# Seven block products for the candidate's input, merged gate tiles, norm sums as side outputs, and some sums on GpSimd

## The chip, the core and the metric

The kernel runs on one core of a Trainium2 chip. The metric is the device time of one execution in microseconds (us). Each version is timed several times; the number given is the median. In the profile PE is TensorE (matmuls), PEld its weight loads, DVE is VectorE, ACT is ScalarE, POOL is GpSimd and SP the engine that issues most DMAs.

## The reference, cut to what matters

The input x has 128 graphs of 64 nodes with 256 features, with a 64x64 adjacency matrix per graph. Four layers follow each other, and each ends in `x = layernorm(x + layer(x))`:

- Layer 0 is a gated graph network of five steps. In each step the node states h are multiplied by a message weight and summed over neighbours (agg), and a gated cell updates h:

```
r = sigmoid(i_r + h_r);  z = sigmoid(i_z + h_z)
n = tanh(i_n + r * h_n)
h = (1 - z) * n + z * h
```

  The i parts are products of agg with the input weights, the h parts are products of h with the state weights. n is called the candidate here.
- Layer 1 sums neighbours, multiplies by W1 (256x1024), divides by the root mean square, applies silu, and multiplies by W2 (1024x256).
- Layer 2 maps x to a tangent space (a logarithm of the norm), sums neighbours, and maps back (a tanh of the norm).
- Layer 3 is an attention with exponentials.

Everything is fp32.

## The kernel before, in words

**Tiling.** Two graphs share the 128 partitions (a block); four blocks make a group of 512 rows, and there are 16 groups. Three sets of work buffers exist (NF = 3), so about three groups are in flight. In layer 0 features lie on partitions, and h and agg are tiles of 128 x 2 x 512: two halves k of the features, and two halves n of the rows (256 columns each).

**Layer 0.** The message weight is multiplied into the input weight beforehand, in the setup, so that a step aggregates h itself (`agg_of`: transposes of h into row layout, a copy hr, the product with the adjacency, a copy agg). The gate products (`gate`) and the state part of the candidate (`state_side`) are 2x2 block products, done with seven block multiplications in the place of eight: sums and differences of weight blocks are prepared in the setup (`sums_of`, tiles w_h, w_a, w_hn with seven blocks), differences of input blocks are made in each step (`sums`, tiles tA for h and tB for agg), and partial results are combined while they leave PSUM. The input part of the candidate is a plain product: `product` into the banks p_in (L675), four products per half, eight per step, 80 steps in all. A bank of p_in is added to r * h_n on VectorE (L837), tanh follows on ScalarE (L839), and three VectorE instructions make the new state hT (L841, L845, L847). This is done for row half 0 first, and for row half 1 later. The gate values live in four tiles of 128x2x256 (slots U, Z, V, R).

**Layer 1.** Seven block multiplications again (`by_sums`, L938 and L943), except in the last two groups, which use the plain product (`as_it_is`). `square` squares each 128x512 piece on ScalarE (L924) and adds it to sqs on VectorE (L926). GpSimd adds the output bias to x (L909, the tile xb).

**Norms.** `layer_norm` runs bn_stats and bn_aggr on VectorE (L685, L686), a power of -0.5 on GpSimd (L690), and a scale and shift on ScalarE or VectorE.

**Order.** Every instruction is first recorded as an operation (`Op`) with an assumed duration, what it reads and what it writes. `Flow.issue` then chooses the order for each engine: it advances a simple clock for each engine and picks the operation that can start first, with ties broken by one of several rules (`ranks`). The kernel before tries all rules in stretches of 37.5 us (10 us near the end) and keeps the 8 (32) best partial plans. Operations with two `ways` may go to ScalarE or VectorE. The orders found are fixed on each engine's queue; at run time the engines only wait on semaphores. Eight PSUM banks are handed out in that order.

Of the kernel before, what the change touches and what calls it, by code (L numbers as in the profile page):

```python
# [42 lines left out]
class Op:  # L43
    __slots__ = ("eng", "us", "run", "ways", "stream", "n", "kb", "sets", "need", "then", "bufs", "opens", "id", "way")

    def __init__(self, ways, stream, n, kb, sets):
        self.ways = {eng: (us, run) for eng, us, run in ways}
        self.eng, self.us, self.run = ways[0]
        self.stream, self.n, self.kb, self.sets = stream, n, kb, sets
        self.need, self.then, self.bufs, self.opens, self.id, self.way = 0, [], (), None, 0, 0.0  # L50


class Plan:


    def __init__(self, flow):
# [8 lines left out]
        self.left, self.first, self.bus, self.done = len(ops), 0, 0.0, 0.0  # L65
        self.lands = [0.0] * flow.TRANSFERS
        self.past, self.order, self.table = None, [], None

    def copy(self):
        c = Plan.__new__(Plan)  # L70
        c.flow, c.need, c.at, c.uses = self.flow, self.need.copy(), self.at.copy(), self.uses.copy()
        c.clock, c.banks, c.lands = self.clock.copy(), self.banks.copy(), self.lands.copy()
        c.queues = [{e: d.copy() for e, d in q.items()} if self.first <= s < self.first + 2 * self.flow.WINDOW else q
                    for s, q in enumerate(self.queues)]
        c.left, c.first, c.bus, c.done = self.left, self.first, self.bus, self.done
        c.past, c.order, c.table = (self.past, self.order), [], self.table
        return c

    def advance(self, until, rank):
# [3 lines left out]
        while self.left and clock["PE"] < until:  # L83
            best = None
            for s in range(self.first, min(self.first + flow.WINDOW, len(self.queues))):
                for e, q in self.queues[s].items():
                    opened = False
                    for _, o in zip(range(flow.AHEAD[e]), q):
                        t = max(clock[e], at[o.id])
# [24 lines left out]
            if eng == "PE":  # L114
                self.done += o.us
# [20 lines left out]

    def bound(self):

        now = self.clock["PE"]
        end = max(now - self.done + self.flow.work, *self.clock.values())  # L140
        for q in self.queues[self.first:]:
            for d in q.values():
                if d:
                    end = max(end, max(self.at[d[0].id], now) + d[0].way)
        return end


class Flow:
# [23 lines left out]
    WINDOW, STRETCH, WIDTH, LAGS = 4, 37.5, 8, (60.0, 150.0,)  # L172


    ENDGAME, LAST_STRETCH, LAST_WIDTH = 400.0, 10.0, 32
# [10 lines left out]
    def op(self, eng, us, run, w=(), r=(), kb=0, sets=None):  # L186
        self.either([(eng, us, run)], w, r, kb, sets)

    def either(self, ways, w, r, kb=0, sets=None):

        o = Op(ways, len(self.streams) - 1, len(self.ops), kb, sets)
# [36 lines left out]
    def ways(self):  # L228
# [9 lines left out]
        self.work = sum(o.us for ops in self.streams for o in ops if o.eng == "PE")  # L238

    def issue(self):  # L240
        self.ways()
        ranks = (lambda s, o: (s, o.n), lambda s, o: (s if o.kb else -s, o.n), *(lambda s, o, lag=lag: (lag * s - o.way, s, o.n) for lag in self.LAGS))
        plans, until = [Plan(self)], 0.0
        while any(p.left for p in plans):
            late = until > self.work - self.ENDGAME
            until += self.LAST_STRETCH if late else self.STRETCH
            found = {}
            for p in plans:
                for rank in ranks:
                    c = p.copy()  # L250
                    if c.advance(until, rank):
                        found.setdefault((round(c.bound(), 3), c.left), c)
            plans = [found[k] for k in sorted(found)[:self.LAST_WIDTH if late else self.WIDTH]]
        p, parts = plans[0], []
        past = (p.past, p.order)
        while past is not None:
            parts.append(past[1])
            past = past[0]
        last = {}
        for part in reversed(parts):  # L260
            for eng, o in part:
                made = o.ways[eng][1]()
                for i in made if isinstance(made, list) else [made]:
                    if eng in last:
                        self.tc.add_manual_dep(i.ins, last[eng].ins.name, self.BEHIND, reason="the plan's order")
                    last[eng] = i
# [3 lines left out]
def kernel(  # L270
# [79 lines left out]
    def dve(n, run, w, r):  # L350
        flow.op("DVE", 0.145 + 0.00105 * n, run, w, r)
# [11 lines left out]
    def scaled(n, o, i, scale, bias, w, r):  # L363

        flow.either([("ACT", 0.22 + 0.00077 * n, lambda: nc.scalar.activation(o(), i(), AF.Identity, bias=bias(), scale=scale())),
                     ("DVE", 0.145 + 0.00105 * n, lambda: nc.vector.tensor_scalar(o(), i(), scale(), bias(), OP.mult, OP.add))], w, r)

    def pool(us, run, w, r=()):
        flow.op("POOL", us, run, w, r)
# [62 lines left out]
    w_a, w_in = [fixed([P, 7, D], f"w_a_{l}") for l in range(L)], [fixed([P, KD, D], f"w_in_{l}") for l in range(L)]  # L432
# [3 lines left out]
    def sums_of(w, eng, us):  # L436

        v = nc.vector if eng == "DVE" else nc.gpsimd
        for o, x0, x1 in ((ms1, ms4, mn22), (ms3, m11, ms4), (ms2, ms1, m11), (ms4, m12, ms2)):
            flow.op(eng, us, lambda o=o, x0=x0, x1=x1: v.tensor_sub(w[:, o, :], w[:, x0, :], w[:, x1, :]),  # L440
                    [(w, o)], [(w, x0), (w, x1)])
# [9 lines left out]
    vecs = fixed([NC, P], "vecs")  # L451
    nmr = fixed([NBLK, P], "nmr")
    at = 0
    for v, n in ((b_ih, NV), (b_hh, NV), (b1, KH), (rms_w, KH)):
        flow.op("POOL", 0.55, lambda v=v, n=n, at=at: nc.gpsimd.dma_start(
            vecs[at:at + n, :], v.rearrange("(c p) -> c p", p=P)), [(vecs, at)], kb=3)
        at += n
    flow.op("POOL", 0.55, lambda: nc.gpsimd.dma_start(nmr.tile(), nodemask.rearrange("(k t) n -> k (t n)", t=2)),
            [nmr], kb=32)
# [694 lines left out]
```

## Time and profile before

| | |
|---|---|
| time, median of 3 | 2415.85 us (2415.77 to 2416.1) |
| span of the profiled execution | 2413.2 us |
| TensorE busy | 2364.1 us, 12098 instructions |
| weight loads busy | 2071.5 us |
| VectorE busy | 1894.3 us, 4404 instructions |
| ScalarE busy | 1211.1 us, 2549 instructions |
| GpSimd busy | 175.1 us, 144 instructions |
| p_in products (L675) | 1280 instructions of 128x256, 321.3 us busy |

How to read it: an fp32 product of the program appears as two matmul instructions in the profile (the 640 products of p_in give 1280). Matmuls overlap in the pipeline, so the mean duration of one (379 ns) is longer than the distance from one to the next. In lists of groups, `out<-in` names the tiles, then come partitions x elements, the count, the busy time, the mean in ns, and the idle time of the engine just before these instructions with the instruction that ended it. In the timeline the first two columns are start and length in us, and a bracket gives idle time and its releaser.

### The profile page before, as it was taken

What the parts mean: (1) busy time and instruction counts of PE and PEld (TensorE: products, weight loads), DVE (VectorE), ACT (ScalarE), POOL (GpSimd) and SP (SyncE); (2) the same over time, 40 slices, a digit from 0 to 9 for tenths busy, and PEclk for the clock granted to TensorE, in tenths of its full rate; (3) what the DMA queues carried; (4) which work ended last, traced back from release to release, by engine and by line L of the source; (5) the groups of instructions that cost most, each with busy time, mean ns of one, the idle gap of its engine ahead of it and who ended that gap; (6) DMA issues with size and microseconds to landing.
All of it is one profiled execution on the core that took longest, in us unless ns stands there. A gap on an engine that the chain in (4) does not pass through costs nothing.

```text
span 2413.2 us, 32774 instructions
## 1 busy us (share of the span) xinstructions
PE 2364.1 (98%) x12098; PEld 2071.5 (86%) x12098; DVE 1894.3 (78%) x4404; ACT 1211.1 (50%) x2549; POOL 175.1 (7%) x144
## 2 busy tenths in 40 slices
PE   9999999999999999999999999999999999999995
PEld 7888888888888888888888888888888888888764
DVE  5677887878869787887977877878697987888766
ACT  3344554545544555555454455455454544555454
POOL 2000000000000000000000000000010000100001
PEclk9999999999999999999999999999999999999997
DMA  3000000000000000000000000000000000000000
GB/s 121 10 9 3 1 29 1 27 3 1 29 1 29 1 18 12 1 29 1 27 3 1 27 3 4 26 1 29 1 18 12 27 3 1 27 10 18 10 9 18
DMA packets 39727, 36.22 MB, mean 15 GB/s; under 512 B 9956, under 2 KB 38656, under 8 KB 39568
## 3 DMA queue, kind: packets, MB, share of 16 engines
q1 hardware_dynamic: 37840, 32.25, 4.2%
q8 instruction: 96, 1.57, 0.3%
q10 hardware_dynamic: 1328, 1.31, 0.2%
q0 software_dynamic: 400, 0.57, 0.1%
q14 instruction: 63, 0.52, 0.1%
HBM read 25.74 MB, written 8.39 MB: 14 GB/s over the span
## 4 chain that ended last, share of the span: by engine, by line
PE 91%; DVE 6%; ACT 1%; issue 1%; POOL 0%; POOLq 0%; ACTq 0%; DVEq 0%
PE p_v L772 11%; PE p_r L772 11%; PE p_w L772 11%; PE p_in L675 11%; PE ps_o L342 9%; PE ps_agg L342 6%; PE p_hy L783 6%; PE p_u L772 6%; PE p_hx L783 4%; PE ps_hr L655 3%; PE ps_a L342 2%; PE p_wh L938 2%; PE p_vh L938 2%; PE p_1h L938 2%; PE ps_sup L342 1%; PE ps_hid L342 1%
## 5 line engine op out<-in xcount | busy, mean ns | idle before, releaser
L675 PE MATMUL p_in<-agg,w_in 128*128 128x256 f32 x1280 | 321.3, 379 | 0.0
L675 PEld LDWEIGHTS p_in<-agg,w_in 128*128 128x128 f32 x1280 | 242.2, 190 | 33.9 <-issue 1.0
L342 PE MATMUL ps_o<-w2s,hid 128*128 128x256 f32 x1024 | 234.0, 381 | 4.8 <-ACT hid L998 4.8
L342 PEld LDWEIGHTS ps_o<-w2s,hid 128*128 128x128 f32 x1024 | 193.8, 191 | 32.4 <-ACT hid L998 5.9
L690 POOL TENSOR_TENSOR rstd<-ve,pow 128x4 f32<-128x4 f32 (+1 forms) x64 | 83.6, 1306 | 1407.3 <-DVE ve L688 1401.3
L826 ACT ACTIVATE V<-V,half_b 128x256 f32<-128x256 f32 x160 | 73.3, 500 | 195.4 <-DVE V L822 195.4
L772 PE MATMUL p_v<-tA,w_h 128*128 128x256 f32 x640 | 170.0, 379 | 0.5 <-DVE V L822 0.5
L772 PE MATMUL p_r<-hT,w_h 128*128 128x256 f32 x640 | 168.5, 379 | 0.0
L772 PE MATMUL p_v<-tB,w_a 128*128 128x256 f32 x640 | 167.1, 379 | 0.0
L772 PE MATMUL p_r<-agg,w_a 128*128 128x256 f32 x640 | 167.0, 380 | 0.0
L794 DVE SCALAR_TENSOR_TENSOR hnb<-p_hy,half_b,hs 128x256 f32<-128x256 f32 x240 | 108.6, 478 | 46.1 <-PE p_hy L783 45.2
L342 PEld LDWEIGHTS ps_agg<-edge,hr 128*128 128x128 f32 x1024 | 136.8, 191 | 8.2 <-ACT hr L360 0.5
L342 PE MATMUL ps_agg<-edge,hr 128*128 128x128 f32 x1024 | 138.7, 275 | 0.0
L360 ACT COPY agg<-ps_agg 128x512 f32<-128x512 f32 x154 | 89.1, 579 | 98.7 <-PE ps_agg L342 98.2
L360 ACT COPY hr<-ps_hr 128x512 f32<-128x512 f32 x125 | 72.2, 578 | 128.2 <-PE ps_hr L655 127.7
L772 PEld LDWEIGHTS p_v<-tB,w_a 128*128 128x128 f32 x640 | 120.7, 190 | 16.1 <-DVE tB L759 0.2
L772 PEld LDWEIGHTS p_r<-agg,w_a 128*128 128x128 f32 x640 | 119.1, 190 | 15.9 <-issue 0.5
L772 PEld LDWEIGHTS p_v<-tA,w_h 128*128 128x128 f32 x640 | 118.4, 190 | 15.9 <-DVE V L822 1.4
L783 PE MATMUL p_hy<-tA,w_hn 128*128 128x256 f32 x480 | 131.3, 380 | 0.0
L772 PEld LDWEIGHTS p_r<-hT,w_h 128*128 128x128 f32 x640 | 116.6, 190 | 14.0 <-PE ps_hr L655 0.5
L826 ACT ACTIVATE Z<-Z,half_b 128x256 f32<-128x256 f32 x160 | 73.8, 503 | 93.4 <-DVE Z L822 93.2
L826 ACT ACTIVATE U<-U,half_b 128x256 f32<-128x256 f32 x160 | 73.3, 500 | 88.9 <-DVE U L822 88.4
(242 smaller groups left out, 5346.9 us busy)
## 6 DMA issues: line engine op xcount, KB each, us to landing
x<-in_x_dram SPq DMA_DIRECT2D x16, 512.0 KB, 3.6
xr<-in_x_dram SPq DMA_DIRECT2D x16, 512.0 KB, 3.5
out_dram<-x_n SPq DMA_DIRECT2D x16, 512.0 KB, 2.9
edge<-in_adj_dram SPq DMA_DIRECT2D x32, 64.0 KB, 2.3
wm<-in_L_gnn_weight_dram SPq DMA_DIRECT2D x5, 256.0 KB, 5.3
w2s<-in_L_gnn_W_dram SPq DMA_DIRECT2D x1, 1024.0 KB, 9.1
w<-in_L_gnn_W_dram SPq DMA_DIRECT2D x2, 512.0 KB, 3.4
w_in_L_gnn_w_hh_dram<-in_L_gnn_w_hh_dram ACTq DMA_DIRECT2D x1, 512.0 KB, 5.2
```

The source lines that it names most:

```text
L342: return nc.tensor.matmul(o, lhsT, rhs, start=(k == 0), stop=(k == nk - 1))
L360: flow.either([("ACT", 0.22 + 0.00077 * n, lambda: nc.scalar.copy(o(), i())), ("DVE", 0.145 + 0.00105 * n, lambda: nc.vector.tensor_copy(o ...
L655: turn(lambda j=j, c=c: nc.tensor.transpose(ps[:, j * D + c * P:j * D + (c + 1) * P], src[:, c, (2 * n + j) * P:(2 * n + j + 1) * P], iden ...
L675: pe(256, lambda c=c, k=k: nc.tensor.matmul(ps[:, c * HR:(c + 1) * HR], w[:, k, c * P:(c + 1) * P], v(k), start=first and c == k == 0, sto ...
L690: pool(1.1, lambda: nc.gpsimd.tensor_tensor(rstd[:, :m, :], ve[:, :m, :], pow2[:, :m, :], OP.pow), [rstd], [ve])
L772: pe(256, lambda i=i, w=w, c=c: nc.tensor.matmul(ps[:, c * HR:(c + 1) * HR], w[:, m, c * P:(c + 1) * P], v[i][0](), start=first and i == 1 ...
L783: pe(256, lambda: nc.tensor.matmul(ps[:, j * HR:(j + 1) * HR], w_hn[:, m, :], v[1][0](), start=first, stop=True, skip_group_check=True), [ ...
L794: dve(300, lambda: nc.vector.scalar_tensor_tensor(o[0](), ps[:, j * HR:(j + 1) * HR], b(c), x[0](), OP.add, OP.add), [o[1]], [ps, x[1], ha ...
L826: act(256, lambda c=c: nc.scalar.activation(o[:, c, :], src(c), AF.Tanh, bias=half_b[:, i * KD + c:i * KD + c + 1], scale=0.5), [(o, c)], ...
L938: pe(256, lambda c=c: nc.tensor.matmul(ps[:, c * HR:(c + 1) * HR], w1f[:, w, (2 * q + c) * P:(2 * q + c + 1) * P], v[0](), start=first and ...
```

## The change

- The input part of the candidate becomes a seven-product block product too (`input_side`): the weights w_in get seven blocks and prepared sums, the banks are p_ix and p_iy, and the partial results are added on VectorE to the tile that holds r * h_n, by instructions that cover one, two or three quarters of it at once. The candidate's tanh and the state update now come once per step, after both row halves are there.
- The four gate tiles are merged into two of 128x2x512 (uu for r and the candidate, uz for z), in the slots U and V; tanh runs over 512 columns for z and the candidate.
- The first two of the four input differences become one 512-column instruction, made for both feature halves at once.
- In all groups but the last two (`summed`), the norms' row sums are side outputs: the addition that makes y also gives its sum (accum_out), ScalarE squares the deviations with a side sum, and bn_stats and bn_aggr go away. The last two groups keep bn_stats and bn_aggr.
- In the same groups the sums of squares of layer 1 and the bias addition of layer 3 move from VectorE to GpSimd (`pool_sum`).
- In the planner, operations can be marked `port`; a marked VectorE or GpSimd operation doesn't start, in the plan, before the last marked one has ended. The search is gone: the file holds a string of 339 rule choices, one for each stretch of 7 us.
- Small tiles move: nodemask and the bias vectors share a tile, the message weights share tiles in pairs, scratch tiles go.

```diff
-                        t = max(clock[e], at[o.id])
+                        t = max(clock[e], at[o.id], self.port) if e in o.port else max(clock[e], at[o.id])
...
+        plan, until = Plan(self), 0.0
+        for c in self.CHOICES:
+            until += self.STRETCH
+            assert plan.advance(until, ranks[int(c)])
...
-w_in = [fixed([P, KD, D], f"w_in_{l}") for l in range(L)]
+w_in = [fixed([P, 7, P], f"w_in_{l}") for l in range(L)]
...
+        def onto_rows(y, b, st, ps, j, scale, x, r):
+
+            def run():
+                return nc.vector.scalar_tensor_tensor(
+                    y[:, b, :], ps[:, j * D:(j + 1) * D], scale(), x[:, b, :], OP.mult, OP.add,
+                    **(dict(accum_out=st[:, b, 0:1]) if summed else {}))
...
+            if summed:
+                dve(4, lambda: nc.vector.tensor_scalar(mv[:, :, 0], st[:, :, 0], -1.0 / D, None, OP.mult), [mv], [st])
+                for b in range(NB):
+                    act(500, lambda b=b: nc.scalar.activation(
+                        o[:, b, :], y[:, b, :], AF.Square, bias=mv[:, b, 0:1], accum_out=st[:, b, 1:2]),
+                        [(o, b), (st, (1, b))], [(y, b), mv])
...
-                for o, x0, x1 in ((of(t1), at(0, 1), at(0, 0)), (of(t2), at(1, 1), of(t1)),
-                                  (of(t3), at(1, 1), at(0, 1)), (of(t4), of(t2), at(1, 0))):
-                    dve(256, lambda o=o, x0=x0, x1=x1: nc.vector.tensor_sub(o[0](), x0[0](), x1[0]()),
-                        [o[1]], [x0[1], x1[1]])
+                dve(512, lambda: nc.vector.tensor_sub(t[:, :2, :], x[:, :, half(1)], blocks_of(x[:, 0, :])),
+                    [(t, t1), (t, t3)], [x], True)
...
+            def input_side():
+
+                px, py = bank("p_ix"), bank("p_iy")
...
+                prod(px, 0, w_in[l], m11, block(0, 0)[0], True)
+                prod(px, 1, w_in[l], m12, block(1, 0)[0])
+                onto(0, 1, lambda: px[:, :HR].unsqueeze(1), px)
+                onto(0, 1, lambda: px[:, HR:].unsqueeze(1), px)
+                prod(py, 1, w_in[l], ms3, sum_of(t3)[0], True)
+                prod(py, 0, w_in[l], ms1, sum_of(t1)[0])
+                onto(3, 1, lambda: py[:, HR:].unsqueeze(1), py)
+                onto(3, 1, lambda: py[:, :HR].unsqueeze(1), py)
+                prod(px, 0, w_in[l], ms2, sum_of(t2)[0])
+                onto(1, 3, lambda: over(px[:, :HR], 3), px)
+                prod(py, 1, w_in[l], mn22, sum_of(t4)[0])
+                prod(py, 0, w_in[l], ms4, block(1, 1)[0])
+                onto(1, 2, lambda: blocks_of(py.tile()), py)
...
-            product(p_in[0], w_in[l], lambda k: agg[:, k, half(0)], True, True, (agg, 0))
-            new_n(0, ur)
+            times_state(0)
...
-            product(p_in[1], w_in[l], lambda k: agg[:, k, half(1)], True, True, (agg, 1))
-            tanh_half(uu, inplace(uu), 0, uu)
-            new_n(1, uu)
-            new_state(1, uu, uv)
+            input_side()
...
-                dve(512, lambda sq=sq: nc.vector.tensor_add(sqs.tile(), sqs.tile(), sq.tile()), [sqs], [sqs, sq])
+            if n and summed:
+                pool_sum(512, lambda: sqt[:, 0, :], lambda: sqt[:, 0, :], sq, [(sqt, 0)], [(sqt, 0), w])
...
-        dve(1030, lambda: nc.vector.tensor_add(x3.tile(), x3.tile(), over(wb_r.tile(), NB)), [x3], [x3, wb_r])
+        if summed:
+            pool_sum(1030, lambda: x3.tile(), lambda: x3.tile(), lambda: over(wb_r.tile(), NB), [x3], [x3, wb_r])
```

## The prediction

> **What bounds the kernel now.** I read the busy shares and the 40 slices first, then the chain that ended last, then busy time by stretch, then the groups by shape, then the timeline around the few gaps of TensorE.
>
> ```profile
> PE 2364.1 (98%) x12098; PEld 2071.5 (86%) x12098; DVE 1894.3 (78%) x4404; ACT 1211.1 (50%) x2549; POOL 175.1 (7%) x144
> PE   9999999999999999999999999999999999999995
> DVE  5677887878869787887977877878697987888766
> PEclk9999999999999999999999999999999999999997
> PE 91%; DVE 6%; ACT 1%; issue 1%; POOL 0%; POOLq 0%; ACTq 0%; DVEq 0%
> ```
>
> TensorE is full in every slice but the last, at full clock, and carries 91% of the chain. So a matmul taken out is worth its full pitch, provided nothing new makes TensorE wait. Where it idles, by stretch (columns: length, busy PE, PEld, DVE, ACT, POOL):
>
> ```profile
> 0.00:2300.00 2300.00, 2285.74 (x11772) 2011.97 (x11773) 1825.75 (x4180) 1155.85 (x2437) 158.72 (x132) 1.00 0.05 15
> 2300.00:2362.50 62.50, 57.40 (x248) 43.78 (x247) 37.98 (x96) 32.38 (x53) 7.02 (x5) 0.97 0.03 9
> 2362.50:2413.20 50.70, 21.00 (x81) 15.78 (x79) 30.62 (x129) 22.87 (x59) 9.35 (x7) 0.69 0.06 21
> ```
>
> Idle: 14.3 us in the first 2300 (2.5 of it before the first matmul), 5.1 in the next stretch, 29.7 in the last, where one group's serial end is left. The reader should see that there is little idle time to win outside the tail.
>
> The mean of a p_in matmul (379 ns) includes pipeline overlap. Its pitch is read from an unbroken run in the chain:
>
> ```profile
> 227.08 13.81 PE ps_o L342 x64
> ```
>
> 13.81 / 64 = 0.216 us per 128x256 instruction; one fp32 product in the program is two of these, 0.432 us.
>
> The repeated gap of the steady part looks like this (start, length):
>
> ```profile
> 336.12 2.38 POOL L909 TENSOR_TENSOR xb<-x_n,b_r 128x1024 f32<-128x1024 f32 x1 [2.49 <-ACT x_n L365]
> ...
> 336.87 2.17 DVE L845 SCALAR_TENSOR_TENSOR hT<-U,hT 128x512 f32<-128x512 f32 x1 [0.52 <-ACT U L826]
> ...
> 337.80 0.73 PEld L938 LDWEIGHTS p_1h<-aggm,w1f 128*128 128x128 f32 x4
> ...
> 339.88 0.42 PEld L655 LDWEIGHTS ps_hr<-ident,hT 128*128 128x128 f32 x4 [1.35 <-PE p_1h L938]
> ```
>
> The state update of L845 lasts 0.69 us elsewhere; beside the GpSimd sum it lasts 2.17, until that ends. The next transposes wait for it: four weight loads from 337.80 are through at 338.66, the next starts at 339.88, 1.2 us lost. In ten of the sixteen groups such a gap of 0.8 to 1.6 us stands beside L909; they sum to 11.2 us, 0.70 us per GpSimd sum.
>
> The tail's gaps:
>
> ```profile
> 2321.01 2.08 PE L342 MATMUL ps_o<-w2s,hid 128*128 128x256 f32 x4 [4.46 <-ACT hid L998]
> ...
> 2370.31 3.78 PE L342 MATMUL ps_sup<-tan,adjT 128*128 128x256 f32 x8 [5.92 <-ACT tan L1046]
> 2384.26 2.16 PE L645 MATMUL ps_T<-ident,x_n 128*128 128x128 f32 x8 [10.16 <-ACT x_n L365]
> ```
>
> **What the Trainium skill says.** (1) "Perfetto Trace Analysis", Identifying the Most-Contended Engine: matmul busy share overstates TensorE, the weight-load share is to be used. Here that is 86%, and a 190 ns load per 216 ns pitch makes 88% the most this stream could show; so TensorE is full. (2) "SBUF — State Buffer", Who interferes with whom: a VectorE instruction with two SBUF inputs and a GpSimd instruction that reads SBUF exclude each other for the whole instruction. The lines above agree (2.17 against 0.69). Instructions with one input in PSUM ran through: at 1359.8, beside L909, two hnb updates took their usual 0.48 each. (3) "GPSIMD Engine Reference", Elementwise: a two-input add takes 1.96 times VectorE's time. Here 2.40 against 1.22 us at 128x1024 (L909, L1103): agrees. (4) "VectorE: DVE Perf Modes", Two Vector instructions with no wait between them: an accumulator output is a second instruction. The setup's five such dots each show one, 81 ns.
>
> **The change part by part.** Rows used for prices:
>
> ```profile
> L675 PE MATMUL p_in<-agg,w_in 128*128 128x256 f32 x1280 | 321.3, 379 | 0.0
> L685 DVE BATCH_NORM_STATS2 st<-y 128x6 f32<-128x256 f32 x192 | 77.0, 401 | 0.1
> L926 DVE TENSOR_TENSOR sqs<-sqs,sq 128x512 f32<-128x512 f32 x112 | 77.1, 688 | 34.8 <-ACT sq L924 33.1
> L837 DVE TENSOR_TENSOR R<-p_in,R 128x512 f32<-128x512 f32 x80 | 55.2, 690 | 3.8 <-PE p_in L675 0.4
> ```
>
> *TensorE.* Per layer and group 8 products become 7; 80 layers lose 80 products, 160 of the 1280 instructions: 160 x 0.216 = **-34.5 us**, all on the path. No other matmul is added; the instruction lists of the two kernels agree in all other shapes.
>
> *VectorE.* Input sums: 160 adds of 128x512 (0.69) go, 110 us; 320 of 256 columns (0.42), 80 of 768 (not in the trace; between 0.69 at 512 and 1.22 at 1024, I take 0.955) and 80 of 512 come: 134 + 76 + 55 = 266. Difference +155. Block differences: 320 of 0.426 become 160 of 0.69: -26. Norms in 14 groups: 224 pairs of statistics and aggregate (0.401 + 0.180) go, 224 accumulator reads (0.081), 56 small means (0.16) and 56 dearer y1 rows (+0.06) come: -99. To GpSimd: 98 square sums (0.688) and 14 sums of 1.22: -84. Small rest -2. Sum **-56**, so about 1838. None of it is on the path by itself: VectorE has some 20% idle. But within the gated layers it rises from about 16.0 to 17.6 us per layer, against 20.6 us of TensorE (42 products x 0.432, 16 instructions of aggregation and 8 transposes at 0.11): still under it.
>
> *ScalarE.* Merged tiles: 640 + 320 tanh calls of 256 columns (434 us by the rows of L826 and L839) become 320 of those (147) and 320 of 512 columns (0.716, as L924 and L998): 376. Deviations squared with a side sum: 224 x (0.383 + 0.194, from L1057) = 129. Net +73, near 1284, 54%: hidden behind TensorE.
>
> *GpSimd.* 98 sums of 128x512: between 0.78 (256 columns, L440) and 2.40 (1024), in line 1.32: 130 us; 14 of 2.40: 34; 16 small weight sums about 0.51: 8, in the setup, beside a TensorE that then works on layer 0. Near 346 us, 14%. What can cost is the lock: 112 new long sums. Below: a gain, if the xb collisions also go, since the new order holds instructions marked for the port back while the other engine has it and can put PSUM work there: -11. Above: 0.70 us each as now. I take -7 net in the steady part: most of the 11 goes, and small unmarked two-input instructions (128x4, the edge masks) meet a lock now and then, some 4 us.
>
> *Longer dependence.* The candidate now needs both halves of agg, its four differences and all seven products before its tanh. Queued behind it on VectorE is the state update, and for that wait the next layer's transposes. One layer's chain is some 26 us (8.6 of gate products, 3.3 of input sums, 4.1 of state updates, the other 10 are copies of 0.58, tanh of 0.5 to 0.72, differences of 1.5, transposes and the first aggregation), while three groups in flight give each layer about 62 us of TensorE work. Taken at 0. Bank count stays: two banks for p_in become p_ix and p_iy.
>
> *Tail.* In the new order group 14's hidden products (128x512, 0.86) stand behind the last transposes of group 15, so the 4.46 gap fills: -4.5. The tanh table load (1.28 us, at 2375.2 on the chain) moves ahead of the last four squares, so group 14's ball factor comes earlier: about -1.5. The last two groups keep the old norms, the rest of the 50.7 us stays. DMA: nodemask goes into another tile and message weights into halves of shared tiles; same count and sizes, hidden in the first 5 us of issue, 0.
>
> Sum against the profile's own span: 2413.2 - 34.5 - 7 - 4.5 - 1.5 = 2365.7. The timed runs lie 2.65 above the profile (2415.85), so **2368 us**.
>
> **Rivals.** *A, the lock (slower).* Each new GpSimd sum stops a VectorE update that TensorE needs next. Scaling 0.70 us by length: 98 x 0.39 + 14 x 0.70 = 48 us, less the 40.5 of matmuls and tail: 2415.85 + 48 - 40.5 = 2423. It decides from 0.36 us of TensorE time per new sum. For: the ten gaps above. Against: those are one collision repeated by an order that knew no lock; some half of VectorE's gated work reads PSUM and runs through. *B, late candidates.* VectorE at 17.6 of 20.6 us in the layers, with locks on top, makes TensorE wait about 0.3 us per layer for p_ix/p_iy sums or hT: 80 x 0.3 = 24 us back, 2392. For: VectorE is busy 46.3 us of the 50 from 1300 on already; against: the layers mix with stages that got lighter. *C, the pitch doesn't fall:* another engine already paces TensorE and the freed 34.5 us turn into idle, 2415. Against: idle of only 14.3 us in 2300.
>
> **How the numbers follow.** Forecast 0.78, own range 2355 to 2384: -11 to +5 for the steady part, some us either way in the tail. B 0.12, A 0.08, C 0.02. Faster: 0.90; C makes 0.02 within 0.2% (4.8 us, about what a measurement can tell from no change); slower 0.08. The range for 8 in 10 takes the forecast's and half of B's: 2353 to 2392.
>
> **What would show it.** Right: about 11940 PE instructions, 1120 in the input products; idle of TensorE before 2260 us no more than now; no L909 gap; VectorE near 1840 us, GpSimd near 350. Wrong: many state updates (hT) or differences (tA, tB) of 1 to 2 us beside GpSimd sums followed by transposes that wait (A); idle before transposes or p_ix/p_iy with short instructions on VectorE (B); a gap in layer 4 or 5 of groups 14 and 15, when only two groups are in flight.

## The result, and the profile after

The changed kernel takes **2398.06 us** (median of 4 runs, 2395.42 to 2399.89) against 2415.97 us for the kernel before (2415.77 to 2417.17), a ratio of 0.9925 (0.9911 to 0.9939). It is faster, by 18 us. The forecast was 47.5 us (2368), with 2353 to 2392 as the range: the sign was right, the size was not.

The page of the changed kernel, its busy shares, the slices and the chain that ended last:

```profile
span 2397.7 us, 32662 instructions
...
PE 2338.0 (98%) x11938; PEld 2045.3 (85%) x11938; DVE 1878.5 (78%) x4291; ACT 1248.8 (52%) x2671; POOL 343.4 (14%) x272
...
PE   9999998999999999999999999999999999999986
...
PEclk9999999999999999999999999999999999999998
...
PE 91%; DVE 5%; ACT 2%; DMA 1%; issue 1%; POOL 0%; ACTq 0%; POOLq 0%; DVEq 0%
```

The 160 matmuls are gone (12098 to 11938) and the clock is as before. Two marks are new: slices of TensorE that aren't full (the seventh and the last but one), and a DMA in the chain, which had none. Busy time of the first 2300 us, in the form shown for the kernel before (length, then PE, PEld, DVE, ACT, POOL):

```profile
0.00:2300.00 2300.00, 2267.07 (x11656) 1993.28 (x11657) 1818.46 (x4091) 1194.11 (x2562) 328.90 (x261) 1.00 0.05 15
```

PE was 2285.74 there. So TensorE idles 18.7 us more in a stretch in which it has less to do.

Busy time hides part of such a gap, since the modelled ends of matmuls overlap. I therefore use starts: from each matmul's start to the next one's, less its pitch (0.216 us for 256 columns, 0.110 for 128, 0.431 for 512). The few instructions of other widths count alike in all runs. The sum of what is left over is called the **loss** below.

| | first matmul | pitches | loss 0 to 50 us | loss 50 to 2250 | loss from 2250 | after the last start |
|---|---|---|---|---|---|---|
| before | 2.5 | 2341.3 | 2.9 | 23.8 | 29.2 | 13.8 |
| after | 2.5 | 2306.8 | 3.0 | 43.9 | 29.6 | 12.1 |

The pitches give back the whole 34.5 us. The steady part then loses 20.1 us more than before, where I had forecast 7 less. The tail (the last two columns), where I had forecast 6 less, comes out 1.3 shorter.

**Where the 20 us went, first half: a wait for the output.** The waits of the changed kernel (us in total, times, longest) have an entry that the kernel before has none of:

```profile
DVE tA L736 <- DMA out_dram<-x_n: 19.3, 6, 5.6
```

The longest of them, in the timeline (start, length, then idle time and releaser) and in the chain:

```profile
1808.98 0.38 SPq L1116 DMA_DIRECT2D out_dram<-x_n  x1
...
1813.67 0.69 DVE L736 TENSOR_TENSOR tA<-hT 128x512 f32<-128x512 f32 x1 [5.61 <-DMA out_dram<-x_n]
...
1816.21 1.22 PE L759 MATMUL p_hy<-hT,w_hn 128*128 128x256 f32 x2 [3.63 <-DVE hnb L779]
```

```profile
1808.73 0.24 ACT x_n L334
...
1808.98 4.57 DMA out_dram<-x_n
...
1813.67 0.69 DVE tA L736
1814.36 0.40 DVE hnb L779
...
1816.21 1.22 PE p_hy L759 x2
```

Norm 3 writes its result to a buffer in slot A. The input differences tA of a later group take the same slot, and may not be written before the transfer of the result has left it. The planner books this transfer with 0.1 us and no bytes (`flow.op("SP", 0.1, ...)`, without `kb`), so it places tA directly behind it. The transfer of 512 KB lands 4.6 us after its issue here, 2.9 us in the median of the page's list of issues. All of VectorE stands still for that time, since tA heads its queue. Behind it waits the VectorE work that TensorE needs next: here the instructions of hnb, which empty the bank that the next state products fill. The Trainium skill ("SBUF — State Buffer", The DMA setup-cost knee) gives a transfer a fixed cost of about 2 us plus its bytes, by its fit 3.2 us for 512 KB as an estimate; the sixteen output transfers of this trace take 2.8 to 4.6.

**Second half: VectorE held by GpSimd's sums.** Groups of VectorE by shape (count, busy, mean ns, idle before), first of the kernel before, then of the changed one:

```profile
L722 DVE TENSOR_SCALAR edge<-edge 64x256 f32<-64x256 f32 x32 | 10.6, 330 | 0.8 <-PE ps_hr L655 0.3
...
L692 DVE SCALAR_TENSOR_TENSOR n<-rstd 128x4 f32<-128x4 f32 x16 | 2.6, 161 | 11.9 <-POOL rstd L690 11.8
```

```profile
L706 DVE TENSOR_SCALAR edge<-edge 64x256 f32<-64x256 f32 x32 | 15.3, 477 | 9.1 <-PE ps_adjT L700 8.4
...
L678 DVE SCALAR_TENSOR_TENSOR n<-rstd 128x4 f32<-128x4 f32 x16 | 5.8, 362 | 14.6 <-POOL rstd L676 14.3
```

Same shapes, same counts, and yet the means go up by half and more: single ones last 1 to 2.3 us. How this reaches TensorE, in the chain around 1932:

```profile
1930.84 1.65 POOL rstd L676
...
1932.51 2.30 DVE n L678
...
1935.79 1.57 ACT x_n L334 x3
1937.36 0.48 ACT aggm L329
...
1937.88 2.50 PE p_1h L940 x5
```

and the GpSimd sum beside it, in the timeline:

```profile
1932.44 2.35 POOL L906 TENSOR_TENSOR xb<-x_n,b_r 128x1024 f32<-128x1024 f32 x1
```

A power on GpSimd ends, VectorE takes its result (an instruction of 128x4, 0.16 us alone), but GpSimd's next instruction, the sum xb of L906 (2.35 us), has started 0.07 us before it. VectorE is held until that sum is over; ScalarE's norm and copy, and then TensorE, come late by as much: 2.4 us of loss. Below, a VectorE instruction counts as **held** when it lasts over 1 us and overlaps a GpSimd sum of 512 or more columns. The trace of the changed kernel has 29 such instructions, that of the kernel before 14, all beside its 16 xb sums. The large state updates and the input differences were marked for the port in the plan; the short instructions and the edge masks were not. The missing marks can't be the whole of it: 16 of the 29 were marked. (The plan is worked out again here from the text of the kernel, and laid beside the trace.)

**The tail** lost its 4.46 us gap before the output products, as forecast, and got another one:

```profile
2281.39 2.06 ACT L334 ACTIVATE x_n<-y,off,rstd 128x256 f32<-128x256 f32 x4
...
2282.03 2.35 PE L311 MATMUL ps_agg<-edge,x_n 128*128 128x128 f32 x11 [4.38 <-ACT x_n L334]
```

Group 14 leaves its gated layer with a norm (eight bn instructions on VectorE, a power, ScalarE). Only two groups are in flight by then. The other one is in its last gated layer, and a gate sum that its last input products wait for stands on VectorE's queue behind those bn instructions (it starts at 2279.86), so it fills the gap with nothing either. Besides, a gap of 2.15 us opens at 2320 before the sums of squares (it ends with sqt of L928), and the last gap, 10.16 us in the kernel before, is 5.75.

### The profile page after: what moved, and what is told of

The parts are those of the page before. It is cut to its first block, busy times and chain, and to the rows that moved or that the text cites. A ratio compares the mean times of both kernels' runs of the same rounds, so it can differ in the third digit from the quotient of the medians.

```text
span 2397.7 us, 32662 instructions
## 1 busy us (share of the span) xinstructions
PE 2338.0 (98%) x11938; PEld 2045.3 (85%) x11938; DVE 1878.5 (78%) x4291; ACT 1248.8 (52%) x2671; POOL 343.4 (14%) x272
## 4 chain that ended last, share of the span: by engine, by line
PE 91%; DVE 5%; ACT 2%; DMA 1%; issue 1%; POOL 0%; ACTq 0%; POOLq 0%; DVEq 0%
PE p_v L753 11%; PE p_w L753 11%; PE p_r L753 11%; PE ps_o L311 9%; PE ps_agg L311 7%; PE p_hy L759 6%; PE p_u L753 6%; PE p_iy L759 6%; PE p_ix L759 4%; PE p_hx L759 4%; PE ps_hr L627 3%; PE ps_a L311 2%; PE p_vh L940 2%; PE p_1h L940 2%; PE p_wh L940 2%; PE ps_wmih L311 1%
## 5 line engine op out<-in xcount | busy, mean ns | idle before, releaser
L807 ACT ACTIVATE U<-U,half_b 128x512 f32<-128x512 f32 (+1 forms) x160 | 93.9, 628 | 133.6 <-DVE U L804 133.4
L759 PE MATMUL p_iy<-tB,w_in 128*128 128x256 f32 x480 | 132.3, 383 | 2.2 <-DVE V L824 2.2
L807 ACT ACTIVATE V<-V,half_b 128x256 f32<-128x256 f32 (+1 forms) x160 | 87.2, 585 | 80.5 <-DVE V L804 80.2
L753 PEld LDWEIGHTS p_r<-hT,w_h 128*128 128x128 f32 x640 | 116.0, 191 | 13.8 <-ACT U L329 0.4
L1000 ACT ACTIVATE hid<-hid,cols 128x512 f32<-128x512 f32 x128 | 85.5, 717 | 62.9 <-DVE hid L998 62.8
L334 ACT ACTIVATE x_n<-y,off,rstd 128x256 f32<-128x256 f32 x173 | 90.8, 589 | 45.4 <-DVE off L680 45.4
```

Source lines behind the costliest of these rows:

```text
L753: pe(256, lambda i=i, w=w, c=c: nc.tensor.matmul(ps[:, c * HR:(c + 1) * HR], w[:, m, c * P:(c + 1) * P], v[i][0](), start=first and i == 1 ...
L759: pe(256, lambda: nc.tensor.matmul(ps[:, j * HR:(j + 1) * HR], w[:, m, :], v[0](), start=first, stop=True, skip_group_check=True), [ps], [ ...
L807: act(256 if len(w) == 1 else 512, lambda: nc.scalar.activation(o(), src(), AF.Tanh, bias=half_b[:, i * KD + c:i * KD + c + 1], scale=0.5) ...
L1000: act(512, lambda v=v, c=c: nc.scalar.activation(v, v, AF.Silu, scale=rmsc(c)), parts, [*parts, cols], SILU)
```

## The experiments

Two theories for the missing 30 us. **T1**: the removed matmuls are worth their pitch, and the loss is (a) the output wait and (b) the held instructions. **T2**: VectorE, which does more per gated layer, is the bound. Rival C of the prediction, that removed matmuls are worth nothing, was tried too. Further theories are named as they come up: **T4**, that an order made to avoid the holds only moves them; **T5**, that the change of time is owed to the longer search; **T7**, that GpSimd's sums run ahead of the plan. From e1 to e5 and in e14 the order on every engine is that of the changed kernel. The medians and ratios stand against runs of the kernel before on the same chip (2415.5 to 2416.7).

| | time, us | ratio to before | loss of TensorE |
|---|---|---|---|
| after | 2398.1 | 0.9925 (0.9911 to 0.9939) | 76.5 |
| e1 own output slot | 2383.2 | 0.9864 (0.985 to 0.9877) | 61.6 |
| e2 sums of 4 columns | 2389.2 | 0.9888 (0.9875 to 0.9902) | 66.6 |
| e3 both | 2369.6 | 0.9808 (0.9795 to 0.9822) | 46.2 |
| e4 a product twice | 2426.4 | 1.004 (1.0025 to 1.0054) | 70.9 |
| e5 sums on VectorE | 2398.0 | 0.9924 (0.9911 to 0.9938) | 75.1 |
| e6 new order | 2380.9 | 0.9854 (0.9839 to 0.9868) | 55.8 |
| e8 new order, sums of 4 columns | 2372.5 | 0.9819 (0.9806 to 0.9833) | 47.3 |
| e9 new order, sums on VectorE | 2389.7 | 0.989 (0.9876 to 0.9903) | 65.3 |
| e7 before, finer search | 2417.1 | 1.0004 (0.9996 to 1.0012) | 55.7 |
| e11 before, finer search, landing known | 2407.2 | 0.9964 (0.995 to 0.9978) | 46.2 |
| e10 new order with a distance | 2413.3 | 0.9988 (0.9981 to 0.9994) | 90.3 |
| e12 as e10, sums really wait | 2377.5 | 0.9842 (0.9828 to 0.9855) | 54.3 |
| **e13 as e6, sums really wait** | **2373.1** | **0.9824 (0.981 to 0.9837)** | 48.1 |
| e14 as e1, sums really wait | 2381.2 | 0.9854 (0.9837 to 0.987) | 58.4 |

**e1, the output wait taken away.** Norm 3 writes into slot U in place of A; the plan still books slot A, so the order stays.

```diff
+            if real:
+                o.make = rows(real, f"x_{name}").make
...
-        o = layer_norm(y3, st3, "A", "n3")
+        o = layer_norm(y3, st3, "A", "n3", real="U")
```

> Order and work are those of the changed kernel; only the last norm's output (the tile that the output DMA reads) lies in slot U of its set in place of slot A, so the next group's differences tA need not wait for that DMA. Theory 1 (the planner counts the output DMA as over after 0.1 us, and five times VectorE stands 2 to 5.6 us in front of L736 until it has landed, which costs TensorE 12.6 us): 2398 - 12 = 2386 us, 2382 to 2390, and no wait of tA for out_dram in the list of waits. Theory 2 (VectorE's load and the longer chain of the candidate make TensorE wait in general): the freed time is lost at the next wait, 2394 to 2400. Rival 3 (the wait moves to the next user of slot U, the z gate of the new group's first layer): also about 2396, with U or V waiting for out_dram.

Measured: 14.9 us less than the changed kernel. The entry of tA and the output is gone from the waits, and DMA from the chain's shares:

```profile
PE 92%; DVE 5%; ACT 1%; issue 1%; POOL 0%; POOLq 0%; ACTq 0%; DVEq 0%
```

One word in the choice of a buffer was worth nearly as much as the whole change had brought.

**e2, the sums made short.** The 98 + 14 new sums work on 4 columns.

```diff
-        pool(0.24 + 0.00211 * n, lambda: nc.gpsimd.tensor_tensor(o(), x0(), x1(), OP.add), w, r)
+        def few(t):
+            return t[:, :, :4] if len(t.shape) == 3 else t[:, :4]
+        pool(0.24 + 0.00211 * n, lambda: nc.gpsimd.tensor_tensor(few(o()), few(x0()), few(x1()), OP.add), w, r)
```

> The 98 sums of squares and 14 bias sums on GpSimd touch 4 columns per row or block in place of 512 or 256 (the rest of these sums is left out, so the norm of layer 1 and the bias of layer 3 are incomplete); order on every engine unchanged. Theory 1 (long GpSimd sums lock out VectorE instructions that the planner did not mark: the edge masks L706 and L896 and the small instructions of the norm and the logarithm; TensorE loses about 14 us by it): 2398 - 14 = 2384 us, 2378 to 2389; no L706 over 0.6 us and no 4-column instruction over 0.4 us except beside the remaining sum L906. Theory 2 (VectorE's load, not the locks): VectorE's work stays as it is, 2394 to 2400. Rival A of the prediction in its full form (0.36 us and more of TensorE per sum): 2398 - 40 or lower.

Measured: 8.9 us less, just past the weak end of what was expected; 7 held instructions are left of 29, beside the xb sums, which stay at full length.

**e3, both edits.**

> Both edits at once: output of the last norm in slot U, and the GpSimd sums on 4 columns (rest left out). Theory 1: the two gains add, 2398 - 26 = 2372 us, 2366 to 2378, about what the removed matmuls alone make of the time before with the same idle time (2416 - 34.5 = 2381) less the gaps that were there before. Theory 2: 2392 to 2400. If the waits only move from one to the other: no better than the better of the two single edits, about 2385.

Measured: 28.4 us less than the changed kernel, some 5 us more than the two alone (14.9 + 8.9). The chain is TensorE's again:

```profile
PE 96%; DVE 2%; ACT 1%; DMA 0%; issue 0%; POOL 0%; ACTq 0%; POOLq 0%; DVEq 0%
```

2369.6 is the forecast within 2 us, and the two causes together are as large as what was missing, in this order of work. That the sum meets the forecast so closely is in part luck: the tail's new gap is still there (4.5 us by starts, before 2252), and the holds of the new sums, for which the forecast had set some 4 us, are all gone.

**e5, the same sums on VectorE**, each in its place of the order.

```diff
-        pool(0.24 + 0.00211 * n, lambda: nc.gpsimd.tensor_tensor(o(), x0(), x1(), OP.add), w, r)
+        pool(0.24 + 0.00211 * n, lambda: nc.vector.tensor_tensor(o(), x0(), x1(), OP.add), w, r)
+        flow.ops[-1].on = "DVE"
```

> The 98 sums of squares (512 columns) and 14 bias sums (1024) are issued on VectorE, at their place in the plan's order, in place of GpSimd; all else unchanged. VectorE gets 98 x 0.69 + 14 x 1.22 = 85 us more work, GpSimd loses about 160, and the locks go. Theory 1 (the loss comes from locks on instructions not marked): a sum takes VectorE 0.69 us where the lock took up to 1.27, so about the same or better, 2385 to 2400. Theory 2 (VectorE is so full in the layers that its load sets the time): clearly worse than the changed kernel, 2410 to 2450.

Measured: no difference. VectorE is busy 52 us longer:

```profile
PE 2342.0 (98%) x11938; PEld 2042.6 (85%) x11938; DVE 1930.7 (81%) x4403; ACT 1251.9 (52%) x2671; POOL 180.5 (8%) x160
```

and TensorE's loss is 75.1 in place of 76.5. T2 falls for this order, in which the wait for the output is still there (18.7 us in the waits of e5). The move to GpSimd bought nothing in this order: what VectorE gained in time was given back, by e2's measure 8.9 us of it in holds.

**e4, an eighth product.** The last product of the input side is issued twice.

```diff
+                pe(256, lambda: [run() for _ in range(1 + twice)], [ps], [(w, m), v[1]])
...
-                prod(py, 0, w_in[l], ms4, block(1, 1)[0])
+                prod(py, 0, w_in[l], ms4, block(1, 1)[0], twice=True)
```

> The changed kernel, every engine's order unchanged, with the last product of the candidate's input side (w_in block ms4) issued twice: 160 more matmul instructions of 128x256, as many as the change took out. The value of that partial result is then doubled, so the output is not the reference's. T1 (a matmul is worth its pitch, the lost gain went into waits): +160 x 0.216 = +34.5 us less what falls into waits that are there anyway (some of the 43.9 us that TensorE loses between 50 and 2250 us), so 2398 + 27 to 35 = 2425 to 2433. Rival C (another engine paces TensorE, so the removed matmuls were worth nothing): 2398, within 5 us.

Measured: 28.4 us more, for 34.5 us of pitch; the loss fell by 5.6 meanwhile. Rival C falls. In this kernel 160 matmuls are worth 28 us, as some of them run while another wait would stand there.

**e6, a new order.** The planner learns of the landing, the edge masks and short instructions get marks, GpSimd's powers lose theirs, norm 3 moves to slot U, some assumed durations are set to measured ones, and the string of choices is found anew. Two places of the edit:

```diff
-        o = layer_norm(y3, st3, "A", "n3")
-        flow.op("SP", 0.1, lambda: nc.sync.dma_start(out_rows[g], o.tile()), (), [o])
+        o = layer_norm(y3, st3, "U", "n3")
+        flow.op("SP", 0.4, lambda: nc.sync.dma_start(out_rows[g], o.tile()), (), [o], kb=512)
...
-                [(ed, t)], [(ed, t)])
+                [(ed, t)], [(ed, t)], True)
```

> The changed kernel with the planner told what the trace showed, and a new string of choices found with it: norm 3 writes to slot U in the place of A; the output transfer counts 512 KB and lands accordingly; the short VectorE instructions with two SBUF inputs, the edge masks and the tan scales are marked for the port; the GpSimd power instructions are not; matmul costs 0.4325 for 256 columns and 0.861 for 512. Same instructions otherwise, the full computation. T1 (output wait and locks on unmarked instructions are what the steady part lost): both are gone without leaving any work out, so about what the version with own output slot and 4-column sums took, 2369.6, with 2360 to 2376 as the range; no wait of tA on an output transfer, VectorE groups L706 and L680 at their lone durations. Rival T4 (the locks are only moved: an order that obeys the port makes VectorE late elsewhere, TensorE waits for it): 2380 or more, no better than the own output slot alone (2383.2).

Measured: 2380.9, so the rival's number and not T1's. There are still 27 held instructions, and all of them are marked ones. For one, at 943 (timeline; two state updates of 0.69 us each beside two sums):

```profile
943.23 1.28 POOL L341 TENSOR_TENSOR sqt<-sqt 128x512 f32<-128x512 f32 x1 [0.84 <-ACT sqt L924]
...
943.41 1.65 DVE L876 SCALAR_TENSOR_TENSOR hT<-U,hT 128x512 f32<-128x512 f32 x1
...
945.09 1.64 DVE L878 SCALAR_TENSOR_TENSOR hT<-hT,V 128x512 f32<-128x512 f32 x1
...
946.78 0.66 PE L627 MATMUL ps_hr<-ident,hT 128*128 128x128 f32 x4 [1.68 <-DVE hT L878]
```

In the plan the two updates were over before the first of these sums began.

**e8, the new order with sums of 4 columns** (the edit of e2 on e6), and **e9, an order searched for sums on VectorE**.

> The replanned kernel (own output slot, marks, new choices), every engine's order unchanged, with the 98 + 14 new GpSimd sums working on 4 columns only; the rest of those sums is left out, so the output is not the reference's. T4 (the planned order keeps sums and state updates apart only on paper; at run time they meet wherever the engines drift by a microsecond): the locks that the trace of the replanned kernel shows (TensorE gaps of 1.8 at 944, 1.7 at 1542, 1.5 at 1801, 1.3 at 2023, 1.9 at 481 and some of the 6 us around 414) go, 2381 - 8 = 2373, range 2369 to 2377. Rival (those gaps stem from the order itself, with VectorE late anyway): 2381, within 3 us.

> The changed kernel with own output slot, the landing of the output known to the planner and the marks, but the 98 sums of squares and the 14 bias additions issued on VectorE, and an order searched for that. The full computation. T1/T4 (the offload buys nothing: what VectorE gains in time it loses in locks): 2376 to 2386, equal to the replanned kernel's 2380.9 within 5 us. Rival T2 (VectorE's 84 us more bind once the waits are gone): 2390 or more. Rival T6 (the locks were the greater cost): 2373 or less.

Measured: e8 8.4 us less than e6, so the sums cost that much even in an order made to avoid the holds. e9 8.8 us more than e6, outside the range of T1 and T4 and just under T2's 2390: with the output wait gone and an order searched for each, VectorE's extra work seems to cost after all. One order was found for each, so a part of the 8.8 us can be the luck of the order.

**e7 and e11, the kernel before with a longer search.** No instruction is changed. e7 has finer stretches and more partial plans; e11 knows the landing of the output as well.

```diff
-    WINDOW, STRETCH, WIDTH, LAGS = 4, 37.5, 8, (60.0, 150.0,)
+    WINDOW, STRETCH, WIDTH, LAGS = 4, 7.0, 450, (60.0, 150.0,)
...
-        flow.op("SP", 0.1, lambda: nc.sync.dma_start(out_rows[g], o.tile()), (), [o])      # e11 alone
+        flow.op("SP", 0.4, lambda: nc.sync.dma_start(out_rows[g], o.tile()), (), [o], kb=512)
```

> The kernel before, no instruction changed, only the search for the order finer: stretches of 7 us in the place of 37.5 and 10, the best 450 partial plans kept in the place of 8 and 32. T5 (part of the changed kernel's 18 us is only its order, searched longer): the kernel before loses 23.8 us of TensorE between 50 and 2250 us, 11 of it beside L909, which its planner does not know; a finer order takes some of the other 13 and of the tail, 2400 to 2412. Rival (the order before was as good as it gets, and the whole change of time is owed to the changed instructions): 2416, within 5 us.

> The kernel before, no instruction changed, with the finer search and with the output transfer's landing (512 KB) known to the planner; new choices found with it. T1 for the old kernel too (the finer search gave nothing because its tighter order ran tA into the output transfer six times, 19.0 us of VectorE waiting): the waits of tA on the output go, TensorE's 2.0 to 3.3 us gaps at 369, 1672, 1793 and 2087 with them, 2400 to 2409. Rival (those gaps come back as others; the order before cannot be improved): 2416, within 4 us.

Measured: e7 the same as before, so T5 falls as it stood; e11 8.7 us less. The waits of e7 and one of them in its timeline point to why the search alone gave nothing:

```profile
DVE tA L757 <- DMA out_dram<-x_n: 19.0, 6, 5.2
```

```profile
1670.20 0.38 SPq L1114 DMA_DIRECT2D out_dram<-x_n  x1
...
1673.20 1.63 DVE L757 TENSOR_TENSOR tA<-hT 128x256 f32<-128x256 f32 x1 [2.67 <-DMA out_dram<-x_n]
```

The tighter order runs into the same unbooked transfer, six times. With the landing known to the planner (e11) the entry is gone from the waits. The fault was in the old planner too; the old, looser order happened not to meet it.

**e10, a distance in the plan.** The plan keeps 1 us between a long sum and a marked VectorE instruction, on either side.

```diff
+    GUARD = 1.0
...
-                        t = max(clock[e], at[o.id], self.port) if e in o.port else max(clock[e], at[o.id])
+                        t = max(clock[e], at[o.id], self.port + (flow.GUARD if e == "POOL" else 0.0)) if e in o.port else max(clock[e], at[o.id])
...
-                self.port = end
+                self.port = end + (flow.GUARD if eng == "POOL" else 0.0)
```

> The replanned kernel (own output slot, landing of the output known, marks; the full computation, same instructions), with one rule more in the planner: 1 us of distance between a long GpSimd sum and a marked VectorE instruction on either side; new choices found with it. T4 (locks return at run time because the engines drift from the plan by up to a microsecond, and cost 8.4 us in the replanned kernel): with the distance most are gone, 2372 to 2377. Rival (drift is larger than 1 us, or the distance makes VectorE late elsewhere): 2381 or more, no gain on the replanned kernel.

Measured: 2413.3, worse than e6 by 32 us, with 58 held instructions. A miss, and the most telling one. I read plan against trace: all 58 are marked, and 54 of them are ones that the plan had put *before* the sum that held them; in e6 it is 10 of 27. (The expectations of e12 and e13 count more widely, 67 of 72 and 16 of 37.) The plan delays a sum until the port is free, but no queue holds that delay: at run time GpSimd starts as soon as its own input is there. The more the plan delays sums, the more they run ahead of it.

**e12 and e13, the delay made real.** In the orders of e10 and e6 each long sum waits, by a semaphore, for the last marked VectorE instruction that the plan put before it.

```diff
+            if eng == "POOL" and o.port and held is not None:
+                self.tc.add_manual_dep(made.ins, held.ins.name, self.BEFORE, reason="the port")
+            if eng == "DVE" and o.port:
+                held = made[-1] if isinstance(made, list) else made
```

> The kernel with the planner's 1 us of distance, same order on every engine, the full computation, with one thing more: each long GpSimd sum really waits, by a semaphore, for the last marked VectorE instruction that the plan put before it. T7 (the plan's wait for the port was on no queue: 67 of the 72 VectorE instructions that were held stood before the sum in the plan): the holds fall from 70 to under 15, and the time from 2413 to 2370 to 2382. Rival T8 (the order itself is bad, VectorE late whatever GpSimd does): 2405 or more, though the holds fall.

> The replanned kernel, same order, the full computation, with the same semaphore wait ahead of each long GpSimd sum. There 16 of 37 held VectorE instructions stood before the sum in the plan. T7: about half of the 8.4 us that the sums cost in this order come back, 2374 to 2379. Rival (the other half, instructions planned after a sum that ended later than planned, carries the cost): 2381, within 2 us. Slower than 2383 if the waits make the sums late for those who need them.

Measured: e12 35.8 us less than e10 with 4 held instructions left; e13 7.8 us less than e6, a little better than T7's range, and equal to e8, in which the new sums were all but left out. The two aren't quite the same test, as e13 makes the xb sums wait as well, which e8 leaves as they are. In e13 17 instructions are still held, every one by a sum that the plan put ahead of it. So the number of holds doesn't give their cost: by these times, nearly all of it lay in this order with sums that ran ahead of the plan. The same place as above, in the timeline of e13 (its line numbers are 5 higher):

```profile
940.10 0.69 DVE L881 SCALAR_TENSOR_TENSOR hT<-U,hT 128x512 f32<-128x512 f32 x1
...
940.83 0.69 DVE L883 SCALAR_TENSOR_TENSOR hT<-hT,V 128x512 f32<-128x512 f32 x1
...
941.57 0.42 PEld L632 LDWEIGHTS ps_hr<-ident,hT 128*128 128x128 f32 x4 [0.18 <-DVE hT L883]
...
945.39 1.27 POOL L346 TENSOR_TENSOR sqt<-sqt 128x512 f32<-128x512 f32 x1 [6.32 <-DVE rd L1116]
```

GpSimd waits 6.32 us for a VectorE instruction, the updates take their 0.69 each and TensorE waits 0.18 in place of 1.68. The delay of the sums hardly reaches TensorE: in the whole of e13 it waits 0.2 us for one of them. e13 does the full computation and is 25 us faster than the changed kernel, 42 us faster than the kernel before.

**e14, the same wait in the changed kernel's own order**, for any VectorE instruction, with norm 3 in slot U.

```diff
+            if eng == "POOL" and o.us > 1.2 and "DVE" in last:
+                self.tc.add_manual_dep(made.ins, last["DVE"].ins.name, self.BEFORE, reason="the port")
```

> The changed kernel's own order and choices, the full computation, norm 3 in slot U (2383.2 alone), and each GpSimd sum of 512 columns or more waits by a semaphore for the VectorE instruction, marked or not, that the plan issued last before it. Leaving the sums out in this order gave 13.6 us (2383.2 to 2369.6). T7 (sums run ahead of the plan here too): 3 to 8 us of these, 2375 to 2380. Rival (in this order the held instructions are the unmarked ones that the plan put beside or behind a sum, which a wait of the sum does not free): 2383, within 2 us. Above 2386 if the waits make the sums late.

Measured: 2.0 us less than e1, the rival's number. Its reason fits only in part. The wait does what it should: in e1 12 of 30 held instructions stood before the sum in the plan, in e14 none of 28 does. The instruction n that the xb sum held for 2.30 us in the changed kernel, for one, runs in its 0.16 us before that sum starts (timeline of e14):

```profile
1915.62 0.16 DVE L683 SCALAR_TENSOR_TENSOR n<-rstd 128x4 f32<-128x4 f32 x1 [1.75 <-POOL rstd L681]
...
1916.00 2.37 POOL L911 TENSOR_TENSOR xb<-x_n,b_r 128x1024 f32<-128x1024 f32 x1 [0.41 <-DVE n L1023]
```

But the sums, once later, hold instructions that the plan put behind them, and 21 of these 28 are marked, so missing marks aren't the main thing. How the 11.6 us between e14 and e3 divide among the held instructions wasn't tried, and why the wait gains so much less in this order than in that of e6 stays open.

## Why the prediction was right and wrong

- **Matmuls, -34.5: right.** The count is exact and the pitches give 34.5 us. Putting 160 back cost 28.4 (e4). The best orders found for the old and the new instructions (e11 and e13) stand 34.1 us apart. That agrees, though it is in part chance: e13's order also knows the port and e11's doesn't, and each is one order found by a search.
- **Steady part, -7: the step that failed.** It came out at +20.1. It had two terms. The gain of 11 from the xb gaps was made in part: of the ten, two are left, but longer ones (1.9 us before 413, 2.4 before 1938). The 4 us for "small unmarked two-input instructions" was mis-sized, and in kind too narrow: the new sums cost 8.9 us (e2) or, with the output wait gone, 13.6 (e1 to e3), and 16 of the 29 held instructions were marked. The prediction took it that the new order "holds instructions marked for the port back"; e10 to e13 show that the plan did so and the queues did not. One of the two edge masks (L706) has only one SBUF input and is held as well; the Trainium skill ("SBUF — State Buffer", Who interferes with whom) lists tensor_scalar among the instructions that can take the shared ports, and the prediction drew only on its line on two inputs. The 14.9 us of the output wait (e1) have no term at all in the prediction. Of DMA it says "same count and sizes, hidden in the first 5 us of issue, 0", and asked of each transfer only whether its data comes in time, not who takes the buffer that it reads. The text of the kernel shows that the output of norm 3 and the tA of a later group share slot A, and that the planner books nothing for that transfer.
- **Tail, -6: failed, -1.3 measured.** The gap of 4.46 closed as forecast, and the last one shrank by 4.4 where 1.5 were forecast. But one of 4.4 opened at 2277, a case that the prediction named ("layer 4 or 5 of groups 14 and 15, when only two groups are in flight") and priced at nothing, and one of 2.15 at 2320.
- **VectorE 1838, measured 1878.5.** With the sums short (e2) it is 1856.9, so some 22 us are time in which the new sums held it; the other 19 weren't traced. GpSimd (346 forecast, 343.4) fits. ScalarE was forecast at 1284 and measured at 1248.8; its own terms add up to +71, not +73. Of the lines at 337.80, the four weight loads are through at 338.53, not 338.66. None of this moves the forecast.
- **Rival A, the lock:** right in kind, wrong in size. The 112 sums cost 8.9 us or 0.08 us each alone, 13.6 us (e1 to e3) with the output wait gone, or 0.12; the rival needed 0.36 to decide. The rule about two SBUF inputs held for the long sums, not for GpSimd's short powers (last section).
- **Rival B, VectorE late:** not in this order (e5), perhaps in an order without the output wait (8.8 us, e9 against e6, one order each). **Rival C:** no (e4).

## What to carry to other kernels

Before you count a moved order as free, ask for every outgoing transfer who writes next to the buffer that it reads, and how far behind: a planner that books it at nothing can put a full engine right behind it, as it did six times here and six times in e7. A rule that exists only in a plan (here, that two engines shall not use a port at once) holds only if something on the queue enforces it; a semaphore on the engine that has time to spare was worth 8 us in one order, 36 in another and only 2 in a third, where the delayed sums met other instructions. And compare two sets of instructions with orders searched equally well, or the order's luck is taken for the change.

## What the runs showed of the hardware

- A VectorE instruction of 128x4 with two SBUF inputs (0.16 us alone) was held for nearly the whole of a GpSimd sum: 2.30 us beside one of 128x1024 (2.35). Its small size didn't shelter it.
- GpSimd's own short instructions of 128x4 and 128x8 (powers, most of them 1.0 to 1.65 us) held no VectorE instruction with two SBUF inputs that started while one ran and no sum did: 68 in the kernel before, for example beside the powers at 1691.65 and 1757.94, and 34 in the changed kernel, all within 0.08 us of their usual time.
- At 1932 a VectorE instruction waited for GpSimd's result and a sum was next on GpSimd: the sum started 0.07 us ahead and held it. The same pair did the same in e1 (1916.89 and 1916.96).
- The output transfer of 512 KB kept its buffer for 2.8 to 4.6 us after its issue, in the waits for it that stand in the chain of the changed kernel.
